# Layer 1 of a four-layer macaron network: gates spread by TensorE row groups, and part of the second mixture's start issued during the attention

## The chip, the cores and the metric

The kernel runs on one core of a Trainium2 chip, in float32. The metric is device time in microseconds (us) of one execution; smaller is better. The engines are TensorE (PE, with its weight loads, PEld), VectorE (DVE), ScalarE (ACT), GpSimd (POOL) and SyncE (SP, which here only issues DMAs). Each has its own instruction queue; they meet at semaphores.

## The reference

The network has four layers. Each is "macaron" shaped: half a feed-forward block, an attention block, half a feed-forward block, all residual, with a layer norm ahead of each. The state x is 4 batches of 512 tokens of 128 values. The feed-forward blocks are mixtures of 8 experts, of four kinds. Only layer 1 is touched by the change. Its mixture is, for normed tokens n:

```
sc   = sigmoid(n @ gate.T)                  # 8 scores per token
m    = the two largest of sc                # top 2
w    = 2.5 * sc[m] / (sum of sc[m] + 1e-20)
y    = sum over the two experts e of w_e * down_e( silu(n @ wg_e.T) * (n @ wu_e.T) )   # inner width 64
y   += the same form with one shared expert of width 128, weight 1
x   += 0.5 * y
```

Its attention is causal, with 16 heads and scores that are the product of two low-rank score matrices (ranks 4 and 8). The same mixture is computed twice, before and after that attention. Layer 2 then follows: a mixture with a linear expert, a gated scan, the mixture again. Layer 3 starts with a mixture that dispatches tokens to experts through DRAM.

## The kernel before

x stays on chip in `xs[b]`, one [128, 4, 128] tile per batch: 128 tokens on the partitions, 4 groups of tokens. Layer 1's mixture computes all 8 experts for all tokens and weighs them by the gates, most of which are zero. Two experts of width 64 fill 128 partitions, so there are `NC` = 4 expert pairs (k = 1 to 4) and the shared expert (k = 0).

`l1_ffn(pool, i, bs)` (L1078) is one mixture for two batches, `bs`; i is 0 for the mixture ahead of the attention and 1 for the one after it. It is a generator: each `yield` is a point at which other work may be put in. Its steps:

- `normed_T` (L1042) norms the batches and turns them with four PE transposes per batch (L187; tile `T_f`), copied to `nT` by ACT (L1049).
- `scored` (L1054, matmul L1058, tile `lg_f`) makes the 8 logits of each token, in groups of 4 small matmuls; ACT makes the sigmoid.
- `up(x, k)` (L1087) makes gate and up projection of one expert pair with two 128x512 matmuls (`gu_f`, L1092 and L1093; each shows as two records), a sigmoid on ACT (L1096) and two products on DVE (L1097, L1098), into a tile `h`.
- `route` and what follows, a chain of small DVE operations, makes `comb`, the weight of each expert for each token (the last step is L1115).
- Tokens must now lie along the free axis, and each expert's weights must be repeated over 64 partitions. `to_rows` (L1067) transposes `comb` to [8, 512] (L1071), copies it out of PSUM with ACT (L1073) and stores it to DRAM (L1075, `rows_f`). Two DMAs per batch (L1124) read it back with a zero step over 64 partitions into `cb` ([128, 4, 512]).
- POOL multiplies each pair's `h` by its slice of `cb` (L1147); `down(k)` (L1132, matmul L1135, tile `o_f`) gathers all five products in PSUM; DVE adds the result to x (L1153).

A mixture takes the batches as two pairs, [0, 1] and [2, 3], whose generators are interleaved by `skewed` with a lag. PE, DVE, ACT and POOL queues are put in order by a scheduler that models the engines, except where the code fixes the order by hand: the attention fixes all four, and the stage after it fixes POOL's. [...]

The first mixture's pair 0 is followed by the begin of the attention for batch 0 (`followed`, L1541): a norm and transposes (`T_a`), matmuls of the low-rank factors (`fac_a`), which go to DRAM and come back rearranged as q and k, and POOL's `k_a` (L1213). The attention (`l1_attn`, L1219) runs 16 units of four heads. When a batch is complete, `ended(b)` adds its projection to x; where a hook `after` is given, its generator for b is then worked off step by step by `go_on`. Before the change layer 1's attention gives no hook.

Behind the attention (`behind`, L1556) each pair runs the second mixture, layer 2's mixture, its scan, its mixture and the start of layer 3's mixture (`f30.tokens`, with indirect DMAs to DRAM on POOL, L408). Layer 2's mixture already spreads its gates with PE: a zeroed tile `l2["gates", …]` is transposed (`gT_f`, L1315), and matmuls of a 0/1 tile with 32 rows (L1346, tile `gate_f`) repeat a row over 128 partitions.

Of the kernel before, what the change touches and what calls it, by code (L numbers as in the profile page):

```python
# [17 lines left out]
P = 128  # L18
# [23 lines left out]
def kernel(ctx: ExitStack, tc: tile.TileContext, a: dict, out: bass.AP):  # L42
# [13 lines left out]
    def bank(name):  # L56
        return psum.tile([P, 512], FP, name=name, tag="bank", bufs=8)
# [954 lines left out]
    def prep_l1():  # L1012
# [26 lines left out]
        l1["wo"] = load_T(a["L1_attn_Wo"], D, D, "wo1T")  # L1039
        l1["bo"] = load_row(a["L1_attn_bo"], "bo1")  # L1040

    def normed_T(pool, bs, tag):  # L1042

        ns = [work.tile([P, NT, D], FP, name=f"n{b}_{tag}", tag="n", bufs=3) for b in bs]
        yield from norms([xs[b] for b in bs], ns, tag, "both")
        nTs = []
        for n, b in zip(ns, bs):
            nT = work.tile([P, S], FP, name=f"nT{b}_{tag}", tag="nT", bufs=4)
            nc.scalar.copy(nT, transposed(n, f"{b}_{tag}"))  # L1049
            nTs.append(nT)  # L1050
        yield
        return nTs

    def scored(nTs, gate, tag):  # L1054

        plg = bank(f"lg_{tag}")
        for t in range(len(nTs) * NT):
            nc.tensor.matmul(  # L1058
                plg[:, t * E : (t + 1) * E],
                nTs[t // NT][:, t % NT * P : (t % NT + 1) * P],  # L1060
                gate,
                start=True,
                stop=True,
            )
        return plg[:, : len(nTs) * NT * E].rearrange("p (g e) -> p g e", e=E)

    def to_rows(pool, gates, i, tag):  # L1067

        pc = bank(f"gT_{tag}")
        for t in range(NT):  # L1070
            nc.tensor.transpose(pc[:E, t * P : (t + 1) * P], gates[:, i * NT + t, :], ident)  # L1071
        gT = pool.tile([E, S], FP, name=f"gT_{tag}", tag="gT")
        nc.scalar.copy(gT, pc[:E, :])  # L1073
        rows = dram.tile([E, S], FP, name=f"rows_{tag}", tag=f"rows_{tag}")
        nc.sync.dma_start(rows, gT)  # L1075
        return rows

    def l1_ffn(pool, i, bs):  # L1078
        tag = f"f1{i}_{bs[0]}"
        G = len(bs) * NT  # L1080
        nTs = yield from normed_T(pool, bs, tag)
        sc = pool.tile([P, G, E], FP, name=f"sc_{tag}", tag="sc1")
        nc.scalar.activation(sc, scored(nTs, l1["gate"], tag), AF.Sigmoid)
        order = [NC] + list(range(NC))
        hs = {}

        def up(x, k):  # L1087
            c = order[k]
            gw = l1["wg"][:, c * P : (c + 1) * P] if c < NC else l1["sg"]
            uw = l1["wu"][:, c * P : (c + 1) * P] if c < NC else l1["su"]  # L1090
            ps = pair(f"gu{c}_{bs[x]}_{tag}")
            nc.tensor.matmul(ps[0], gw, nTs[x], start=True, stop=True)  # L1092
# [5 lines left out]
            nc.vector.tensor_tensor(h, h, ps[1], ALU.mult)  # L1098
# [12 lines left out]

        comb = pool.tile([P, G, E], FP, name=f"comb_{tag}", tag="comb")
        nc.vector.tensor_tensor(comb, m1, m2, ALU.add)
        nc.vector.scalar_tensor_tensor(comb, comb, 2.5, sc, ALU.mult, ALU.mult)
        nc.vector.tensor_tensor(comb, comb, bc(total, [P, G, E]), ALU.mult)  # L1115
        up(0, 1)
        yield
        cbs = []
        for x, b in enumerate(bs):
            rows = to_rows(pool, comb, x, f"{b}_{tag}")  # L1120

            cb = pool.tile([P, NC, S], FP, name=f"cb{b}_{tag}", tag="spread", bufs=4)
            for u in range(2):
                nc.sync.dma_start(  # L1124
                    cb[u * I1 : (u + 1) * I1],
                    bass.AP(tensor=rows.tensor, offset=rows.offset + u * S, ap=[[0, I1], [2 * S, NC], [1, S]]),
                )
            cbs.append(cb)
        for x, b in enumerate(bs):
            po = bank(f"o{b}_{tag}").rearrange("p (t d) -> p t d", d=D)  # L1130

            def down(k):  # L1132

                for t in range(NT):
                    nc.tensor.matmul(  # L1135
                        po[:, t, :],
                        hs[x, k][:, t * P : (t + 1) * P],
                        l1["down"][order[k]],
                        start=(k == 0 and t == 0),
                        stop=(k == NC and t == NT - 1),  # L1140
                    )

            for k, c in enumerate(order):
                if (x, k) not in hs:
                    up(x, k)
                if c < NC:
                    nc.gpsimd.tensor_tensor(hs[x, k], hs[x, k], cbs[x][:, c, :], ALU.mult)  # L1147
                if k > 1:
                    down(k - 2)
                yield  # L1150
            down(NC - 1)
            down(NC)
            nc.vector.scalar_tensor_tensor(xs[b], po, 0.5, xs[b], ALU.mult, ALU.add)  # L1153
            yield
# [61 lines left out]

        return begin, fetch, project, future, {}

    def l1_attn(beside, begun):  # L1219
        begin_, fetch_, project_, future, early = begun  # L1220
        with tc.tile_pool(name="attn1", bufs=2) as pool:
            def begin(b):
                if b == 1:
                    vpads[1] = padded(pool, 1)
                if b > 0:
                    yield from begin_(b)

            def fetch(b, g):
                if (b, g) not in early:
                    fetch_(b, g)  # L1230

            def project(b, g):
                return early[b, g] if (b, g) in early else project_(b, g)

            def residual(b, po):
                nc.vector.tensor_tensor(xs[b], po, xs[b], ALU.add)

            attention(pool, "a1_", begin, project, residual, l1["wo"], lambda h: future, None,
                beside(pool), fetch,
            )  # L1240

# [222 lines left out]
    def whole(parts):  # L1464
        for _ in parts:
            pass
# [57 lines left out]
    with tc.tile_pool(name="weights12", bufs=1) as mid:  # L1524
# [9 lines left out]
        nc.scalar.activation(first, l2["m"][:, 0, 0:1], AF.Sigmoid)  # L1534
        for b in range(NB):
            whole(f01.combine(b))
        with tc.tile_pool(name="ahead1", bufs=2) as ahead:
            vpads[:] = [padded(ahead, 0), None]
            begun = l1_begin(ahead)

            def followed(pool, bs):  # L1541
                yield from l1_ffn(pool, 0, bs)
# [12 lines left out]

        def behind(pool, bs):  # L1556
            yield from l1_ffn(pool, 1, bs)
            yield from l2_ffn(pool, 0, bs)
            yield from l2_attn(pool, bs)
            yield from l2_ffn(pool, 1, bs)  # L1560
            if bs[0] == 0:

                parts = f30.tokens(bs, l3["gate"], "scalar", pool, apart=True)
                while next(parts, "end") != "end" and next(parts, "end") != "end":
                    yield
            else:
                yield from skewed([f30.tokens([b], l3["gate"], "scalar", pool) for b in bs], 3)
# [72 lines left out]
```

## Time and profile before

| What | Value |
|---|---|
| Runs | 1504.74, 1509.73, 1515.06 us; median 1509.73 |
| Profiled execution | 1513.06 us; span 1511.3 us; mean granted PE clock 0.91 |
| PE busy | 1271.2 us (84%) |
| DVE busy | 880.3 us (58%) |
| POOL busy | 694.0 us (46%) |
| ACT busy | 682.8 us (45%) |
| First mixture of layer 1 | about 443 to 513 us of the span |
| Attention of layer 1 | about 515 to 740 us |
| Second mixture of layer 1 | about 740 to 830 us |
| Rest of the stage behind the attention | up to about 1010 us |

The profile is that of one execution. Its page gives the busy time of each engine, groups of instructions (line, engine, operation, tile written and tiles read, how many, busy time, mean of one, and idle time ahead of them with what ended it), and a chain of waits: from the last instruction back to what released it, step by step. "issue" in that chain is time in which an engine waited for nothing that the profile shows. Windows give the busy time of each engine in a stretch, with the clock granted to PE (1.00 is full).

### The profile page before, as it was taken

What the parts mean: (1) busy time and instruction counts of PE and PEld (TensorE: products, weight loads), DVE (VectorE), ACT (ScalarE), POOL (GpSimd) and SP (SyncE); (2) the same over time, 40 slices, a digit from 0 to 9 for tenths busy, and PEclk for the clock granted to TensorE, in tenths of its full rate; (3) what the DMA queues carried; (4) which work ended last, traced back from release to release, by engine and by line L of the source; (5) the groups of instructions that cost most, each with busy time, mean ns of one, the idle gap of its engine ahead of it and who ended that gap; (6) DMA issues with size and microseconds to landing.
All of it is one profiled execution on the core that took longest, in us unless ns stands there. A gap on an engine that the chain in (4) does not pass through costs nothing.

```text
span 1511.3 us, 28774 instructions
## 1 busy us (share of the span) xinstructions
PE 1271.2 (84%) x10645; PEld 816.7 (54%) x10645; DVE 880.3 (58%) x2890; ACT 682.8 (45%) x1431; POOL 694.0 (46%) x808
## 2 busy tenths in 40 slices
PE   4787999995969999999878878729689999998394
PEld 3465666774746666667555656616433333333173
DVE  5236767763355657767456566525367787774343
ACT  1235877871422367767522222103236655564042
POOL 5346767871433678868323111464431223312343
PEclk9897999995999999999999888759879999999597
DMA  9410240002513884231022000023105000000223
GB/s 262 101 53 22 79 170 12 9 7 73 151 37 65 223 258 145 87 121 44 4 64 49 1 1 1 28 71 91 60 15 177 15 7 10 14 3 15 78 78 112
DMA packets 100660, 106.21 MB, mean 70 GB/s; under 512 B 9084, under 2 KB 73832, under 8 KB 100520
## 3 DMA queue, kind: packets, MB, share of 16 engines
q1 hardware_dynamic: 91752, 90.11, 20.7%
q0 software_dynamic: 6656, 13.22, 2.5%
q8 instruction: 84, 1.38, 0.4%
q10 hardware_dynamic: 2112, 1.05, 0.3%
q14 instruction: 56, 0.46, 0.1%
HBM read 62.49 MB, written 41.85 MB: 69 GB/s over the span
## 4 chain that ended last, share of the span: by engine, by line
PE 70%; DVE 9%; POOL 8%; DMA 5%; issue 5%; ACT 3%; SPq 1%; POOLq 0%; ACTq 0%; DVEq 0%
PE s_a L610 13%; PE t_a L655 10%; PE o_f L515 6%; PE h_f L479 6%; PE acc_a L677 5%; PE acc_a L749 5%; PE y_f L1329 3%; PE t_a L610 3%; POOL disp_f L408 2%; PE ot_a L768 2%; PE gu_f L1092 2%; PE lg_f L322 1%; POOL rstd_f L165 1%; DVE low L699 1%; PE gu_f L1093 1%
## 5 line engine op out<-in xcount | busy, mean ns | idle before, releaser
L642 POOL TENSOR_SCALAR sc_a<-sc_a,top_a 128x128 f32<-128x128 f32 (+3 forms) x256 | 274.8, 1089 | 84.7 <-DVE top_a L627 55.8
L610 PE MATMUL s_a<-k_a,q_a 32*128 32x512 f32 (+3 forms) x1536 | 263.4, 544 | 7.0 <-DVE top_a L631 3.7
L719 ACT ACTIVATE w_a<-t_a 128x512 f32<-128x512 f32 x256 | 140.4, 595 | 116.6 <-PE t_a L610 86.9
L699 DVE TENSOR_REDUCE low<-s_a 128x1 f32<-128x512 f32 x256 | 163.4, 684 | 45.4 <-PE t_a L610 32.7
L655 PE MATMUL t_a<-ident,sc_a 128*128 128x128 f32 x1280 | 174.3, 283 | 4.3 <-DVE top_a L631 3.8
L610 PE MATMUL t_a<-ql_a,k_a 32*128 32x512 f32 x512 | 167.2, 644 | 0.3 <-DVE low L699 0.2
L501 POOL DMA_INDIRECT res_f<-y_f,back_f x112 | 109.8, 980 | 124.6 <-ACT y_f L500 90.3
L655 PEld LDWEIGHTS t_a<-ident,sc_a 128*128 128x128 f32 x1280 | 144.6, 144 | 41.0 <-issue 16.5
L644 ACT ACTIVATE sc_a<-sc_a,top_a 128x128 f32<-128x128 f32 (+3 forms) x256 | 135.0, 575 | 12.8 <-DVE top_a L631 12.2
L610 PEld LDWEIGHTS s_a<-k_a,q_a 32*128 32x128 f32 x1536 | 91.5, 187 | 79.1 <-issue 41.9
L664 ACT ACTIVATE w_a<-t_a 128x256 f32<-128x256 f32 (+2 forms) x192 | 94.2, 526 | 71.0 <-PE t_a L655 70.8
L408 POOL DMA_INDIRECT disp_f<-n_f,to_f x96 | 94.8, 988 | 56.2 <-issue 35.8
L515 PE MATMUL o_f<-w_l,h_f 128*128 128x128 f32 (+1 forms) x896 | 109.6, 277 | 0.0
L515 PEld LDWEIGHTS o_f<-w_l,h_f 128*128 128x128 f32 (+1 forms) x896 | 102.1, 184 | 8.0 <-DVE back_f L464 4.4
L479 PE MATMUL h_f<-dT_f,w_l 128*128 128x320 f32 (+1 forms) x256 | 104.1, 544 | 2.8 <-ACT dT_f L457 2.8
L677 PE MATMUL acc_a<-w_a,vpad 128*32 128x128 f32 x2560 | 98.2, 280 | 0.0
L666 ACT COPY w_a<-t_a 128x256 f32<-128x256 f32 (+2 forms) x192 | 93.5, 527 | 5.0 <-PE t_a L655 4.7
L631 DVE CUSTOM_DVE_ANT_0 sc_a<-s_a,future 128x128 f32<-128x128 f32 (+3 forms) x128 | 62.3, 487 | 47.7 <-PE s_a L610 39.0
L1147 POOL TENSOR_TENSOR h_f<-h_f,cb_f 128x512 f32<-128x512 f32 x32 | 40.7, 1286 | 104.4 <-DVE h_f L1098 62.7
L631 DVE CUSTOM_DVE_ANT_0 sc_a<-s_a,table 128x128 f32<-128x128 f32 (+3 forms) x128 | 62.3, 487 | 43.5 <-PE s_a L610 38.3
L500 ACT ACTIVATE y_f<-o_f,d_f 128x128 f32<-128x128 f32 (+1 forms) x112 | 39.0, 394 | 98.0 <-DVE o_f L495 94.1
L749 PE MATMUL acc_a<-w_a,vpad 128*32 128x256 f32 x1024 | 82.1, 391 | 1.0 <-DVE low L699 0.9
(341 smaller groups left out, 2182.8 us busy)
## 6 DMA issues: line engine op xcount, KB each, us to landing
fac_a<-fac_a_sb SPq DMA_DIRECT2D x36, 256.0 KB, 4.9
disp_f<-zeros_f SPq DMA_DIRECT2D x4, 2080.0 KB, 10.6
d_f<-disp_f SPq DMA_DIRECT2D x32, 260.0 KB, 3.0
w_l<-in_L_ffn_w_dram SPq DMA_DIRECT2D x16, 512.0 KB, 7.2
cb_f<-rows_f SPq DMA_DIRECT2D x16, 512.0 KB, 8.4
q_a<-fac_a SPq DMA_DIRECT2D x32, 256.0 KB, 3.5
k_a<-fac_a SPq DMA_DIRECT2D x32, 256.0 KB, 3.8
r_f<-res_f SPq DMA_DIRECT2D x16, 256.0 KB, 2.8
```

The costliest lines, as they stand in the source:

```text
L408: nc.gpsimd.indirect_dma_start(out=self.to[c][i0 + t][:, :], out_offset=bass.IndirectOffsetOnAxis(ap=to[:, c, t : t + 1], axis=0), in_=ns[ ...
L479: nc.tensor.matmul(ps[u][:, :cap], w1[:, e, (c + u) * P : (c + u + 1) * P], dT, start=True, stop=True)
L515: nc.tensor.matmul(po[:m, s, :], h[:, c, s * P : s * P + m], w2[:, e, c, :], start=(c == 0), stop=(c == NC - 1),)
L610: nc.tensor.matmul(ps[:, n0:n1], q[r : r + SLOT, i * P : (i + 1) * P], k[r : r + SLOT, n0:n1], start=True, stop=True)
L631: nc.vector.tensor_tensor_reduce(sc, banks[r][:, :n], more, -1.0, HUGE, ALU.add, ALU.min, top)
L642: nc.gpsimd.tensor_scalar(sc, sc, top, None, ALU.subtract)
L644: nc.scalar.activation(sc, sc, AF.Exp, bias=top, scale=-1.0)
L655: nc.tensor.transpose(ps[:, x * n + j * P : x * n + (j + 1) * P], st["sc", u, i, r0 + x][:, j * P : (j + 1) * P], ident,)
L677: nc.tensor.matmul(st["acc", u][r * SLOT : (r + 1) * SLOT, i * P : (i + 1) * P], vpads[b % 2][:, j, g * 4 + r, :], st["w", u, i, r][:, j * ...
L699: nc.vector.tensor_reduce(st["low", u][:, i, c : c + 1], ps, AX.X, ALU.max, negate=True)
L719: nc.scalar.activation(w, ps, AF.Exp)
L749: nc.tensor.matmul(acc[r * SLOT : (r + 1) * SLOT, n0:n1], vpads[b % 2][:, j, g * 4 + r, :], st["w", u, j, r][:, n0:n1], start=(j == 0 and ...
```

## The change

It has two parts.

The gates of layer 1 are spread by PE instead of a trip through DRAM. The last product of the gate chain is written into a zeroed tile `gates` [128, 8, 128], in which expert e = 2r + u has column 32r + u. `spread(x)` transposes the four [128, 128] blocks of a batch into one bank, ACT copies it to `gT` [128, 512], four matmuls with 32 rows each, one in each of PE's row groups, multiply `halves` (a tile of zeros and ones) by `gT` into four banks, and four ACT copies fill `cb`. It is issued for the pair's first batch ahead of the loop over batches, and for the second at k = 2 of the first batch's loop. The first mixture has a new `gates` tile of its own, zeroed by DVE; the second uses layer 2's. `halves` is built once in a preamble. The stores of rows and the broadcasts go.

The second mixture's pair 0 gets its norms, transposes, `nT` copies and logits in `l1_early`, which runs through the attention's hook for b = 1. Its generator then starts at the sigmoid, with the logits in an SBUF tile that DVE copied from PSUM.

```diff
@@ prep_l1
+        halves = pools["w"].tile([P, P], FP, name="halves", tag="halves")
+        for u in range(2):
+            flag = small.tile([P, 1], FP, name=f"half{u}", tag=f"half{u}", bufs=1)
+            nc.vector.tensor_reduce(flag, ident.rearrange("p (r c) -> p r c", c=SLOT)[:, :, u], AX.X, ALU.add)
+            nc.vector.tensor_copy(halves[:, u * I1 : (u + 1) * I1], flag.to_broadcast([P, I1]))
+        l1["halves"] = halves
...
-    def to_rows(pool, gates, i, tag):
...
+    def l1_early(bs, got):
+        tag = f"f11_{bs[0]}"
+        ns = [work.tile([P, NT, D], FP, name=f"n{b}_{tag}", tag="n", bufs=3) for b in bs]
+        yield from norms([xs[b] for b in bs], ns, tag, "both", True)
+        nTs = []
+        for n, b in zip(ns, bs):
+            yield
+            nT = work.tile([P, S], FP, name=f"nT{b}_{tag}", tag="nT", bufs=4)
+            copy(nT, transposed(n, f"{b}_{tag}"))
+            nTs.append(nT)
+            yield
+        lg = small.tile([P, 2 * NT, E], FP, name=f"lg_{tag}", tag="lg_early", bufs=1)
+        for x in range(len(bs)):
+            yield
+            nc.vector.tensor_copy(lg[:, x * NT : (x + 1) * NT], scored(nTs[x : x + 1], l1["gate"], f"{x}_{tag}"))
+        got[:] = nTs, lg
+
-    def l1_ffn(pool, i, bs):
+    def l1_ffn(pool, i, bs, gates, early=None):
-        nTs = yield from normed_T(pool, bs, tag)
+        if early:
+            nTs, lg = early
+        else:
+            nTs = yield from normed_T(pool, bs, tag)
+            lg = scored(nTs, l1["gate"], tag)
...
-        nc.vector.tensor_tensor(comb, comb, bc(total, [P, G, E]), ALU.mult)
+        parted = gates.rearrange("p g (r c) -> p g r c", c=SLOT)[:, :, :, : E // 4]
+        four = [P, G, 4, E // 4]
+        nc.vector.tensor_tensor(
+            parted, comb.rearrange("p g (r u) -> p g r u", r=4), total.unsqueeze(2).unsqueeze(3).to_broadcast(four), ALU.mult
+        )
...
-            rows = to_rows(pool, comb, x, f"{b}_{tag}")
-            cb = pool.tile([P, NC, S], FP, name=f"cb{b}_{tag}", tag="spread", bufs=4)
-            for u in range(2):
-                nc.sync.dma_start(
...
+        def spread(x):
+            tag_x = f"{bs[x]}_{tag}"
+            pc = bank(f"gT{tag_x}")
+            for t in range(NT):
+                nc.tensor.transpose(pc[:, t * P : (t + 1) * P], gates[:, x * NT + t, :], ident)
+            gT = pool.tile([P, S], FP, name=f"gT{tag_x}", tag="gT2", bufs=2)
+            nc.scalar.copy(gT, pc)
+            cbs[x] = pool.tile([P, NC, S], FP, name=f"cb{tag_x}", tag="spread", bufs=3 + i)
+            banks = [bank(f"cb{r}_{tag_x}") for r in range(NC)]
+            for r in range(NC):
+                rows = slice(r * SLOT, (r + 1) * SLOT)
+                nc.tensor.matmul(banks[r], l1["halves"][rows, :], gT[rows, :], start=True, stop=True)
+            for r in range(NC):
+                nc.scalar.copy(cbs[x][:, r, :], banks[r])
+
+        spread(0)
...
                 if k > 1:
                     down(k - 2)
+                if k == 2 and x + 1 < len(bs):
+                    spread(x + 1)
                 yield
@@ l1_attn
-            attention(pool, "a1_", begin, project, residual, l1["wo"], lambda h: future, None,
+            attention(pool, "a1_", begin, project, residual, l1["wo"], lambda h: future, after,
@@ the stages
+        early = []
...
+                gates = pool.tile([P, 2 * NT, P], FP, name="gates", tag="gates", bufs=1)
+                nc.vector.memset(gates, 0.0)
                 whole(skewed([followed(pool, bs) for bs in pairs], 12))
-            l1_attn(lambda pool: prep_l3_ffn(xs[0]), begun)
+            l1_attn(lambda pool: prep_l3_ffn(xs[0]), begun, lambda b: l1_early(pairs[0], early) if b == 1 else iter(()))
...
-            yield from l1_ffn(pool, 1, bs)
+            yield from l1_ffn(pool, 1, bs, l2["gates", bs[0]], early if bs[0] == 0 else None)
```

More of the change, by code (lines that the diff above doesn't have):

```diff
@@ L1065, in scored @@
         return plg[:, : len(nTs) * NT * E].rearrange("p (g e) -> p g e", e=E)
-    def to_rows(pool, gates, i, tag):
[L1069 to L1076, printed above, removed]
-    def l1_ffn(pool, i, bs):
+    def l1_early(bs, got):
[15 more added lines that the diff above has]
+    def l1_ffn(pool, i, bs, gates, early=None):
         tag = f"f1{i}_{bs[0]}"
         G = len(bs) * NT
-        nTs = yield from normed_T(pool, bs, tag)
+        if early:
[3 more added lines that the diff above has]
+            lg = scored(nTs, l1["gate"], tag)
         sc = pool.tile([P, G, E], FP, name=f"sc_{tag}", tag="sc1")
-        nc.scalar.activation(sc, scored(nTs, l1["gate"], tag), AF.Sigmoid)
+        nc.scalar.activation(sc, lg, AF.Sigmoid)
         order = [NC] + list(range(NC))
@@ L1114, in l1_ffn @@
         nc.vector.scalar_tensor_tensor(comb, comb, 2.5, sc, ALU.mult, ALU.mult)
-        nc.vector.tensor_tensor(comb, comb, bc(total, [P, G, E]), ALU.mult)
+        parted = gates.rearrange("p g (r c) -> p g r c", c=SLOT)[:, :, :, : E // 4]
[3 more added lines that the diff above has]
+        )
         up(0, 1)
         yield
-        cbs = []
-        for x, b in enumerate(bs):
-            rows = to_rows(pool, comb, x, f"{b}_{tag}")
-            cb = pool.tile([P, NC, S], FP, name=f"cb{b}_{tag}", tag="spread", bufs=4)
-            for u in range(2):
-                nc.sync.dma_start(
[L1125 to L1128, printed above, removed]
+        cbs = {}
+        def spread(x):
[13 more added lines that the diff above has]
+        spread(0)
         for x, b in enumerate(bs):
@@ L1217, in l1_begin, with l1_attn @@
         return begin, fetch, project, future, {}
-    def l1_attn(beside, begun):
+    def l1_attn(beside, begun, after):
         begin_, fetch_, project_, future, early = begun
@@ L1541, in followed @@
             def followed(pool, bs):
-                yield from l1_ffn(pool, 0, bs)
+                yield from l1_ffn(pool, 0, bs, gates)
                 if bs[0] == 0:
```

## The prediction

> **What bounds the kernel now.** I read the page first, then the waits of the spread gates, then the chain of waits in the two stretches with layer 1's mixtures, then busy time by stage.
>
> ```profile
> PE 1271.2 (84%) x10645; PEld 816.7 (54%) x10645; DVE 880.3 (58%) x2890; ACT 682.8 (45%) x1431; POOL 694.0 (46%) x808
> ...
> L1147 POOL TENSOR_TENSOR h_f<-h_f,cb_f 128x512 f32<-128x512 f32 x32 | 40.7, 1286 | 104.4 <-DVE h_f L1098 62.7
> ...
> cb_f<-rows_f SPq DMA_DIRECT2D x16, 512.0 KB, 8.4
> ```
>
> ```profile
>   DMA cb_f<-rows_f: 41.6, 3
> ```
>
> TensorE (PE) is the fullest engine, so a gain must remove PE time or PE gaps. POOL's multiply by the spread gates waited for the DMA three times, 41.6 us together; listed singly these were 17.9 us at 464.5 (first mixture), 19.0 at 761.7 and 4.7 at 798.3 (second). POOL has half its time free, so what counts is PE beside these waits.
>
> ```profile
> 450.10 3.83 issue
> 453.93 1.29 PE gT_f L1071 x8
> ...
> 493.45 0.87 PE gu_f L1092 x2
> 496.62 1.15 issue
> 497.77 3.75 POOL h_f L1147 x3
> ...
> 512.91 1.57 POOL h_f L1147
> 514.48 1.23 POOL k_a L1213
> 515.76 1.43 PE s_a L610 x16
> ```
>
> ```profile
> 746.76 4.41 issue
> 752.55 1.46 DMA rows_f<-gT_f
> 754.67 6.85 DMA cb_f<-rows_f
> 761.68 3.71 POOL h_f L1147 x3
> ...
> 791.43 6.77 DMA cb_f<-rows_f
> ...
> 826.96 1.07 PE gate_f L1346 x8
> ```
>
> ```profile
> 454.00:510.00 56.00, 55.57 (x264) 35.49 (x264) 32.25 (x69) 14.83 (x26) 19.98 (x17) 0.97 0.54 138
> ...
> 746.00:752.00 6.00, 1.57 (x8) 0.62 (x7) 4.83 (x21) 0.61 (x2) 0.00 (x0) 0.96 0.00 0
> 752.00:760.00 8.00, 7.93 (x24) 3.78 (x22) 3.01 (x5) 2.85 (x5) 0.00 (x0) 0.82 0.53 135
> 760.00:772.00 12.00, 5.93 (x35) 5.36 (x36) 3.52 (x7) 1.65 (x4) 7.47 (x8) 0.86 0.42 89
> ```
>
> The columns of the last fence are the stretch, its length, busy PE, weight load, DVE, ACT, POOL, then the granted clock. The first mixture (first chain) never shows the DMA: from 454 to 510 PE is busy 55.57 of 56 us, because expert pairs' up-projections were queued ahead of the waiting down-projections. In the second mixture (second chain) the DMA stands on the path twice, 1.46 + 6.85 and 1.43 + 6.77 us, and PE has gaps. Added over 746 to 850, PE is busy 87.5 of 104 us; in the 5-us slices clocks of 0.5 to 0.86 cost about 6 us of the busy time. So some 22 us there are overhead.
>
> **What the Trainium skill says.** "TensorE: Matmul & The Clock Gate", "Measured speedup vs the span model": four row-tiled matmuls (K=32, N=512) are 3.07 times as fast as one by one. The trace agrees: the next layer's gate spread does it, four matmuls (eight records) in 1.07 us in the chain at 826.96, against 3.44 for eight records at the 0.86 per two of L1092. The same page, "What's actually happening": after an idle window of about 3.4 us PE's clock is halved until a busy window has passed. Agrees: after 4.41 us idle a 128x512 matmul took 1.06 us per record against 0.59, and the 5-us slice from 750 had clock 0.66. "TensorEngine Tiling (Array Packing)", "PSUM Bottleneck": after row tiling, the copies out of PSUM may become the bottleneck. Here four ACT copies of 0.6 us follow 1.07 us of matmul; no row of before shows that pressure. "DMA: Bandwidth & Descriptors", "Anatomy of one DMA", puts about 2 us of fixed cost on a DMA, mostly its completion; here 16 KB took 1.46 us and 512 KB 6.85.
>
> **The change, part by part.**
> *Spread by PE.* Removed: 8 stores of rows and 16 broadcasts, 24 issues of SP (0.28 and 0.62 us each; SP is idle enough to count this as zero; the cover is its free queue). Added per batch: the four transposes stay four (0.44 us), but now fill 128 rows; the ACT copy of gT stays 0.57 to 0.60 us; four matmuls 1.07 us; four more ACT copies, 4 x 0.6 = 2.4 us. Over 8 batches PE gets 8.6 us, ACT 19 us. ACT is busy 27 to 33% in the mixtures, so its 19 us is hidden behind PE; without that cover it would be 9.6 per mixture. PE's 4.3 us per mixture lie on the path wherever PE is full. A new wait comes too: PE is served in order, and the four matmuls wait for the gT copy; for each pair's first batch they stand right behind the transposes, with up-projections queued after. That is 0.6 us of copy and two hand-overs, an estimate of 0.8 to 1 us each, twice per mixture; in the second batch a down-projection stands between. The new zeroed gate tile is one DVE memset of 128x1024, at most the 0.92 us POOL takes for the like tile, before the mixture opens. The 0/1 weights are four small DVE instructions (0.25 us) in a preamble: zero, under PE's expert work there.
>
> *First mixture.* No DMA wait is on its path, so nothing is gained by removing it. What ends it is the start of the attention: factor matmuls fac_a (495.0) to DRAM and back to q/k, landed at about 512.8, then k_a on POOL (514.48), first score 515.76. In PE's instruction order before, fac_a stands ahead of the third batch's down-projections; after, these, the spread's matmuls and the fourth batch's come ahead of it. Counting PE's instructions at the durations above, fac_a moves to about 504.5, 9.5 us later. The way from fac_a to q/k, 17.8 us, should lose a little because the 512 KB transfers are gone from it: I take 2. Value +7.5 us; bounds +2.3 (only 4.3 us of PE less 2 us of gap) and +9.
>
> *Moved into the attention.* Norms already ran there. Moved: 8 transposes (0.87), 16 score matmuls (1.70), two nT copies (1.2 of ACT or DVE), two small DVE copies (0.5); no DMA. From 660 to 700 PE is busy 10 of 10, so 2.57 us is on the path if it finds no gap; later in the attention there are small gaps (4.2 of 5 at 700). Bounds 0 and +3; value +1.5.
>
> *Second mixture.* Two accounts. (a) Path: 16.5 us of DMA (sum of the four legs) give way to two times copy 0.6 + matmul 1.07 + copy 0.6 = 4.5, so −12. (b) PE: work of 87.5 us loses the moved 2.6 and gains 4.3, so 89.2; of 22 us overhead about 8 go: the wait of 759.9 to 763 and part of 766 to 772, where batch 0's residual (771.7) moves to about 766, and the half clock after it. What stays: the gate chain on DVE. The sigmoid can start at once, but DVE still has the last residual and the flags of the next layer ahead of it, so the gates are ready only about 1.5 us sooner than 751.07, and PE runs dry at about 743.6 (740.15, the end of the last projection, and four up-projections' 0.86) instead of 746.8, having nothing else. That gives −8 + 1.7 = −6.3. Value −10, nearer the path's because the first multiply comes at about 752 instead of 761.7 and batch 1's at 785 to 790 instead of about 800; bounds −3 and −14.
>
> *After it.* Pair 0 leads, so POOL's queue order changes: pair 0's six dispatch DMAs (L408) for the last layer's mixture (0.99 us each) come ahead of pair 2's norm instead of after. From 850 to 1010 PE is busy 110.8 of 160, so a shift can go either way: 0, bounds −5 and +5.
>
> Sum: 7.5 + 1.5 − 10 + 0 = −1. Against the profiled execution's own 1513.06 us (span 1511.3 and 1.76 around it) that is 1512; this execution lies 3.3 above the median of 1509.73, so I forecast 1509.
>
> **The rivals.**
> *R1: the whole gain arrives.* fac_a's delay is absorbed (POOL waits at 497.77 and 515 to 533 anyway for its own scores) and the second mixture follows its path: 0, +1.5, −14, tail −4: −16.5, 1493. For: 41.6 us of waits vanish and 8.4 MB of traffic. Against: PE's 55.57 of 56 in the first mixture.
> *R2: PE's queue stalls at each spread.* The matmuls wait for the gT copy, which stands on ACT behind sigmoids and earlier spread copies, and everything on PE waits behind them, fac_a among it; POOL then waits, and the next down-projections too. Place: the eight spreads. Price: at 2 us each 16 us, on top of −1 gives +15, 1525; 1% is reached from about 2 us per spread. For: the order puts nothing between transposes and matmuls for each pair's first batch. Against: ACT's low load.
> *R3: the change doesn't do what it says,* the row groups run one after another: 0.86 each, 3.44 per batch instead of 1.07, 8 x 2.4 = 19 us: 1528. Against: the 1.07 us of the same form.
>
> **How the numbers follow.** Forecast (within 1%, which is 15 us, about what a measurement of this kernel tells from no change) 0.62; R1 0.23; R2 0.12; R3 0.03. Adding the ends of the parts gives −20 to +17 around the median, 1490 to 1527; all ends falling together is unlikely, so the range takes R1's and R2's times as its ends: 1493 to 1525. R1 is the faster case, R2 and R3 the slower.
>
> **What would show it.** Right: no wait for a DMA in POOL's multiply; spreads of about 1.07 us; the attention's first score 5 to 9 us later relative to the mixture's start; batch 0 of the second mixture done within 27 us of the last projection instead of 31.5; PE's busy sum up by about 9 us. Wrong: fac_a not later, or the first scores where they were (R1); PE gaps of 2 us ahead of spread matmuls (R2); matmuls at 0.86 apart (R3); or a tail that shifts by over 5 us.

## The result, and the profile after

The changed kernel takes 1520.29 us (median of 13 runs) where the kernel before, on the same chip, takes 1513.35. The ratio is 1.0049, with a 95% interval of 1.0031 to 1.0067: about 7 us slower. The forecast was no change (1509 us). The sign was not forecast, and the parts of the sum were further off than their total.

The profiled execution has a span of 1518.7 us, 7.3 more than before. First, lines of its page: busy time by engine, and the group of POOL's products by the spread gates.

```profile
PE 1282.6 (84%) x10709; PEld 821.8 (54%) x10709; DVE 880.8 (58%) x2898; ACT 700.8 (46%) x1464; POOL 696.0 (46%) x808
...
L1178 POOL TENSOR_TENSOR h_f<-h_f,cb_f 128x512 f32<-128x512 f32 x32 | 40.8, 1275 | 112.4 <-DVE h_f L1116 58.1
```

PE has 11.4 us more to do and ACT 18.0. The second view is that of the spread gates' tile: who works on it, and what POOL waited for.

```profile
L1155 PE MATMUL cb_f<-gT_f,halves x64: 587/692/1218, 457.8 to 805.9; 32*128 32x512 f32 x64
L1157 ACT COPY cb_f<-cb_f x32: 563/592/617, 459.9 to 808.0; 128x512 f32<-128x512 f32 x32
...
  POOL h_f L1178: 31.0, 3
```

POOL's wait for the DMA is gone; in its place stand three waits, 31.0 us together, which ACT's copies end. They are not the price of the copies: of the 31.0 us some 19 had passed before DVE had made the gates, and the rest was transposes, copies and matmuls, each wait ending with the first copy of 0.6 us.

The chain of waits through the first mixture, to set beside the one shown of before:

```profile
452.32 3.74 issue
456.06 1.10 PE gT_f L1148 x4
457.82 2.09 PE cb_f L1155 x8
...
499.64 1.11 PE cb_f L1155 x8
500.75 1.07 ACT cb_f L1157 x3
...
510.55 1.73 PE fac_a L1211 x4
...
522.02 3.67 DMA k_a<-fac_a
526.16 0.88 issue
527.04 1.27 POOL h_f L1178
```

The spread's matmuls are now links of that chain, the attention's factors (`fac_a`) come at 510 instead of 495, and their way through DRAM ends it. The same for the second mixture:

```profile
753.61 4.62 issue
759.65 2.09 PE cb_f L1155 x8
761.74 2.00 PE gu_f L1110 x2
...
768.84 2.03 ACT cb_f L1157 x4
773.03 1.27 POOL h_f L1178
774.42 1.27 POOL h_f L1178
776.11 1.68 POOL rstd_f L165
```

The wait for the gates is still there, 4.62 us where it was 4.41, and no DMA follows. (The view calls it "issue"; DVE finished the gates at 758.1, and PE's transposes of them began at 758.2.) But the chain still passes through POOL.

Four marks divide the two traces: the first score matmul of the first mixture, the attention's first score, its last projection, and the last product of layer 2's two mixtures (`y_f`). In us:

| Stretch | before | after | difference |
|---|---|---|---|
| up to the first mixture | 444.6 | 445.1 | +0.5 |
| first mixture, to the attention's first score | 71.2 | 82.0 | +10.8 |
| attention, to its last projection | 224.4 | 223.0 | −1.4 |
| then to the last `y_f` | 236.5 | 231.4 | −5.2 |
| then to the end | 534.7 | 537.1 | +2.5 |

Each column is one execution. The stretch to the last `y_f` holds the second mixture of layer 1 and layer 2's two; in the last stretch no instruction was changed.

### The profile page after: what moved, and what is told of

Read it like the earlier page. It is cut to its first block, busy times and chain, and to the rows that moved or that the text cites. A ratio compares the mean times of both kernels' runs of the same rounds, so it can differ in the third digit from the quotient of the medians.

```text
span 1518.7 us, 28895 instructions
## 1 busy us (share of the span) xinstructions
PE 1282.6 (84%) x10709; PEld 821.8 (54%) x10709; DVE 880.8 (58%) x2898; ACT 700.8 (46%) x1464; POOL 696.0 (46%) x808
## 3 DMA queue, kind: packets, MB, share of 16 engines
q10 hardware_dynamic: 2112, 1.05, 0.3%
## 4 chain that ended last, share of the span: by engine, by line
PE 69%; DVE 10%; POOL 7%; DMA 5%; issue 5%; ACT 3%; SPq 1%; POOLq 0%; DVEq 0%; ACTq 0%
PE s_a L610 13%; PE t_a L655 9%; PE o_f L515 6%; PE h_f L479 6%; PE acc_a L677 5%; PE acc_a L749 4%; PE t_a L610 3%; PE y_f L1362 2%; POOL disp_f L408 2%; PE ot_a L768 2%; PE lg_f L322 1%; POOL rstd_f L165 1%; PE o_f L1166 1%; PE T_f L187 1%; PE gu_f L1110 1%
## 5 line engine op out<-in xcount | busy, mean ns | idle before, releaser
L610 PEld LDWEIGHTS s_a<-k_a,q_a 32*128 32x128 f32 x1536 | 92.4, 188 | 77.2 <-issue 41.9
L164 POOL TENSOR_SCALAR rs_f<-mv_f 128x4 f32<-128x4 f32 (+1 forms) x23 | 5.5, 239 | 185.1 <-DVE mv_f L161 184.6
```

Source lines behind the costliest of these rows:

```text
L610: nc.tensor.matmul(ps[:, n0:n1], q[r : r + SLOT, i * P : (i + 1) * P], k[r : r + SLOT, n0:n1], start=True, stop=True)
```

## The experiments

Ratios are against the kernel before in runs on the same chip, with 95% intervals; 0.1% is 1.5 us. Two of the four groups of runs (e5 to e8, e13 to e16) fell on two other chips, where the kernel before takes 1535 and 1536 us. The same instructions between the last projection and the last `y_f` took some 12 us longer there (243.5 in e7 against 231.4 in the changed kernel). For the first 219 us of that stretch PE's instructions in these two traces agree within 0.5 us; then comes one stall, which is described at the end. So times inside that stretch are compared over chips only up to the first `y_f`. Ratios differ over chips as well: e8 and e12 are the same kernel and gave 0.9938 and 0.9891. A difference of that size between ratios from different chips is not taken as shown.

### The two parts apart: e1, e2, e3, e5

The theory at this point was the result's own table: the first mixture loses, the second gains, and the early start is small. e1 keeps the spread in the first mixture alone, e2 in the second alone with the early start, e3 has the early start alone, e5 the spread in the second mixture alone. The edit is the same in all, a choice by mixture:

```diff
-        spread(0)
+        if i in SPREAD:                  # (0,), (1,) or ()
+            spread(0)
+        else:
+            for x, b in enumerate(bs):
+                rows = to_rows(pool, comb, x, f"{b}_{tag}")
...
-            l1_attn(lambda pool: prep_l3_ffn(xs[0]), begun, lambda b: l1_early(pairs[0], early) if b == 1 else iter(()))
+            l1_attn(lambda pool: prep_l3_ffn(xs[0]), begun, None)      # e1 and e5
```

> PE spreads the gates in the first mixture only; the second keeps its DMAs, and nothing is moved into the attention. Both theories put the loss into the first mixture, so both expect its first attention score 10 to 12 us later than before (about 526 to 528 of the span instead of 515.8), and the end of the attention about as much later. If the whole of it stays to the end, the kernel is 8 to 12 us slower than before. A rival, that the loss is absorbed by the attention or by the tail, expects less than 4 us.

> PE spreads the gates in the second mixture only, with the early start in the attention; the first mixture is as before. Theory: the first mixture is the loser and the rest a gain. First score at 515 to 517, end of the attention 0 to 2 us earlier than before, the last linear-expert product of layer 2's first stage earlier by about 5 us relative to it, the kernel 4 to 8 us faster than before. Rival: the gain in the second mixture is eaten by the stages after it; then within 2 us of before.

> The early start in the attention alone; both mixtures spread their gates by DMA as before. Expected: the attention's end within 2 us of before (the moved 2.6 us of PE find gaps), the gates of the second mixture's first pair ready about 2 us earlier after the last projection, and the DMA wait after them as long as before, so 1 to 3 us faster. Rival, moved work lies on the attention's full PE: 0 to 2 us slower.

> PE spreads the gates in the second mixture only, and nothing is moved into the attention: the fourth corner of a square whose others are the kernel before, the early start alone and the two together. Theory: the early start and the spread hide the same DMA wait, so alone the spread gains where together it lost 5 us: from the last projection to the last product of layer 2's first stage 229 to 233 us instead of 236.5, the kernel 3 to 7 us faster than before. Rival: the spread costs its PE time whether the wait is exposed or not: 237 to 242 us there, and the kernel 0 to 5 us slower than before.

| Run | first mixture | early start | second mixture | ratio | interval |
|---|---|---|---|---|---|
| e1 | PE | no | DMA | 1.0105 | 1.0076 to 1.0134 |
| e2 | DMA | yes | PE | 0.9974 | 0.9962 to 0.9987 |
| e3 | DMA | yes | DMA | 0.9925 | 0.9901 to 0.9948 |
| e5 | DMA | no | PE | 1.0024 | 1.0006 to 1.0042 |
| changed | PE | yes | PE | 1.0049 | 1.0031 to 1.0067 |

The first mixture was the loser, as expected, and by more: +1.05% alone, 16 us. (Of the 16.0 us between e1's trace and that of before, 9.8 lie in the first mixture and 3.9 behind the last `y_f`, where no instruction differs; why is open.) e2 came out at the lower edge of what was expected. e3 was the miss that turned the study: the part that I had valued at nearly nothing gains 11 us, and e2 against e3, on one chip, says that the PE spread loses 0.49%, 7 us, in the second mixture as well. Their traces agree: from the last projection to the last `y_f` e2 takes 231.2 us, e3 223.7. e5 went to the rival: even where the DMA's wait was exposed, the spread costs 0.24% (3.6 us). From e2 to the changed kernel the first mixture's spread adds 0.75%, where alone it cost 1.05%; what makes that difference is open.

Why nothing came of removing 16.5 us of DMA shows in e5's chain of waits through the second mixture:

```profile
754.58 4.49 issue
...
760.54 2.09 PE cb_f L1171 x8
762.63 2.00 PE gu_f L1123 x2
...
773.86 1.27 POOL h_f L1205
775.55 1.68 POOL rstd_f L165
...
778.34 1.27 POOL h_f L1205
```

After 4.5 us without work PE's clock is low, and the spread takes 2.09 us instead of 1.07 (this is the halving that the Trainium skill describes in "TensorE: Matmul & The Clock Gate", "What's actually happening"). PE then waits 0.68 us for the copy of the transposed gates, and later on POOL's products, between which stands the next pair's norm, as before. In the 100 us after the last projection PE is idle 14.9 us with e5 and 16.7 before; the spread's own 5.2 us more than fill the difference. The first `y_f` comes 92.4 us after the last projection; before it was 90.9.

e11, e3's kernel once more, shows the other side. The first line is POOL's wait for the gates, over both mixtures; then come pieces of the chain of waits through the second:

```profile
  DMA cb_f<-rows_f: 54.4, 4
```

```profile
739.78 4.55 issue
...
746.02 1.46 DMA rows_f<-gT_f
...
748.14 7.16 DMA cb_f<-rows_f
755.46 4.96 POOL h_f L1199 x4
760.85 1.67 POOL rstd_f L165
```

The 54.4 us are not a longer wait than the 41.6 of before: 15.3 of them belong to the first mixture, which is unchanged, and the same wait of before, 15.4 us, is put down to DVE by the view. In the second mixture POOL waits 16.5 and 4.9 us for the DMA, where it waited 19.0 and 4.7. So these waits are nearly all still there, and the kernel is 1% faster. The chain view still lists the DMA, but PE has no gap of 0.1 us from 744.3 to 763.5: while POOL waits, PE makes the second batch's up-projections. Here is PE in the 100 us after the last projection, before and e11 (stretch, length, busy time with records, granted clock, DMA share, GB/s):

```profile
740.15:840.15 100.00, 83.26 (x428) 0.93 0.20 43
```

```profile
736.33:836.33 100.00, 88.36 (x484) 0.95 0.20 44
```

### What sets the first mixture's end: e4, e6, e7, e9

The prediction's theory: the factors fall behind other work in PE's queue, and their way through DRAM sets the first score. The rival: PE's own account (spread matmuls, waits, low clock). e4 and e6 start pair 2 later, which lets the factors pass; e9 begins the attention for batch 0 as soon as that batch leaves the mixture; e7 doubles the spread's matmuls.

```diff
-                whole(skewed([followed(pool, bs) for bs in pairs], 12))
+                whole(skewed([followed(pool, bs) for bs in pairs], 20))      # e4; 16 in e6
```

```diff
+            for _ in range(2 if i == 0 else 1):                              # e7
                 for r in range(NC):
                     nc.tensor.matmul(banks[r], l1["halves"][rows, :], gT[rows, :], start=True, stop=True)
```

```diff
-                yield from l1_ffn(pool, 0, bs, gates)                        # e9
-                if bs[0] == 0:
-                    yield from begun[0](0)
...
+                ffn = l1_ffn(pool, 0, bs, gates)
+                yield from skewed([ffn, attention_begins()], 0) if bs[0] == 0 else ffn
```

> The changed kernel with the second pair of the first mixture started 20 steps behind the first instead of 12, so that PE's queue has the factor matmuls of the attention's first batch ahead of the third batch's down-projections. Theory of the prediction (the late factor chain sets the first score): factor matmuls some 10 us earlier than in the changed kernel, first score at 517 to 519, kernel 8 us faster than the changed one. Rival (PE's own account sets it: spread matmuls, waits behind the gT copy, slow clock): the factors come earlier too, but the first score only by 2 to 3 us, at 523 to 525, and the kernel is 2 to 3 us faster than the changed one.

> The changed kernel with the second pair 16 steps behind, which puts the factor matmuls just after the fourth spread and ahead of the third batch's waiting down-projections. Theory of the prediction (the factor chain sets the first score): first score 8 to 10 us earlier than in the changed kernel, relative to the mixture's first score matmul at 72 to 74 us instead of 82. Rival (PE's own account, with the factor chain worth only the last gap of 2.7 to 3.8 us): 78 to 82 us, and the kernel within 4 us of the changed one.

> The changed kernel with the four spread matmuls of each batch done twice in the first mixture (the second time over the first's result): one cost doubled, 4 times 1.07 us more of PE. If PE's account sets the first mixture's end, the first score comes 4 to 5 us later and the kernel is 4 to 5 us slower than the changed one. If copies on ACT, POOL or the factor chain set it, PE has slack and both move by less than 2 us.

> The changed kernel with the attention's begin for batch 0 started as soon as that batch leaves the first mixture, so that PE's queue has the factor matmuls ahead of the third spread; lag and pairs stay. Theory of the prediction (the factor chain sets the first score): factors at some 45 to 50 us after the mixture's first score matmul instead of 65, first score at 72 to 74 us instead of 82. Rival (PE's own account): factors as early, but the first score at 78 to 80 us, 2 to 4 us better than the changed kernel, since only the last gap of 2.7 us ahead of the first score goes.

From the mixture's first score matmul, in us:

| | factors | attention's first score | ratio to before |
|---|---|---|---|
| before | 50.4 | 71.2 | 1 |
| changed | 65.3 | 82.0 | 1.0049 |
| e4 | 50.9 | 91.2 | 1.0087 |
| e6 | 64.8 | 90.3 | 1.0127 |
| e7 | 71.5 | 88.9 | 1.0088 |
| e9 | 50.2 | 90.3 | 1.0088 |

e4 and e9 have the factors where they were before the change, and the first score is 8 to 9 us later still than in the changed kernel. So early factors are not sufficient, against the prediction's theory, but the rival did not forecast this either. e9's timeline tells why (start, duration, instruction, and in brackets the idle time ahead of it with what ended it). ACT and DVE first, then POOL, then PE:

```profile
511.17 0.65 ACT L1116 ACTIVATE h_f<-gu_f 128x512 f32<-128x512 f32 x1
516.75 0.69 DVE L1249 TENSOR_TENSOR q_a<-q_a,q_a 128x512 f32<-128x512 f32 x1 [3.70 <-DMA q_a<-fac_a]
517.36 0.68 DVE L1117 TENSOR_TENSOR h_f<-h_f,gu_f 128x512 f32<-128x512 f32 x1
...
514.82 1.26 POOL L1249 TENSOR_TENSOR k_a<-k_a,k_a 128x512 f32<-128x512 f32 x1 [6.08 <-DMA k_a<-fac_a]
518.92 1.27 POOL L1249 TENSOR_TENSOR k_a<-k_a,k_a 128x512 f32<-128x512 f32 x1 [2.84 <-DVE h_f L1118]
520.14 2.49 POOL L1180 TENSOR_TENSOR h_f<-h_f,cb_f 128x512 f32<-128x512 f32 x2
...
521.46 2.08 PE L1168 MATMUL o_f<-wd1T,h_f 128*128 128x128 f32 x8 [7.70 <-POOL h_f L1180]
...
538.17 0.48 PE L610 MATMUL s_a<-k_a,q_a 32*128 32x128 f32 x2
```

Once the factors are early, the attention's products come earlier in their engines' queues, too: `q_a` on DVE, `k_a` on POOL. They wait there for their DMAs, and the mixture's products stand behind them. The costly wait was DVE's: a sigmoid that ACT had done at 511.8 got its product on DVE only at 517.4, behind `q_a`; POOL's `k_a` then took 1.3 us more, and PE waited 7.7 us. The factors themselves were no longer the limit: `k_a` was done at 520.2, while PE worked on the mixture without a gap from 521.5 until the first score at 538.2. In e4, too, `k_a` was done at 514.4 and the first score began at 532.8, right behind other work of PE. In e6 the lag delayed the second pair so much that the factors came no sooner; it says nothing on the question.

e7 answers more directly: 4.3 us more of matmuls (at 1.07 us per batch at full clock) move the first score by 6.9 us. Of these, 2.7 had come before the first doubled spread: it began 15.4 us after the mixture's first score matmul instead of 12.7, in an execution whose granted clock up to there was 0.61 instead of 0.75. The other 4.2 are the matmuls' own, so PE has no slack. (The time's 0.39%, 6 us, is taken over two chips.)

The clock is a rival for each difference of a few us here, since each trace is one execution. e3 and e11 are the same kernel, and in both the first mixture is that of before; it took 76.4 and 70.9 us, at a granted clock (the number after the bracket) of 0.89 and 0.98:

```profile
447.50:523.90 76.40, 71.05 (x315) 0.89 0.48 121
```

```profile
443.20:514.10 70.90, 65.28 (x314) 0.98 0.52 130
```

But at 0.98 the first mixture took 71.2 us before and, with the spread, 81.0 in e1, so the spread's loss is not the clock's. The changed kernel's trace shows where it lies. To the end of all its down-projections but the last, PE needs 79.3 us; before, all were done in 71.1. In that, 5.2 us are spread matmuls and 1.4 us two waits behind the copy of the transposed gates; the up-projections took 38.0 us instead of 36.1, and three gaps for POOL's products cost 1.9 where one cost 1.3. In e1 the up-projections took 36.0 us, and the same point came at 77.1. Only then comes a wait for `k_a`, 2.7 us (3.8 in e1), the factors' own share. What stays open is the share of the late factors in a kernel in which DVE's and POOL's order is undisturbed: no run had that.

### Why the early start gains: e10, e13, e14, e15, e16

The early start takes 3 us off the way to the second mixture's gates and 2.6 us of PE off the mixture, yet gains 11 us and more. e10 tested whether the order of up-projections is it, by issuing the second batch's first two ahead of the first batch's downs, in the kernel before:

```diff
+                if i == 1 and x == 0 and k == 0:
+                    for later in range(2, NC + 1):
+                        up(0, later)
+                    up(1, 0)
...
+                if i == 1 and x == 0 and k == 2:
+                    up(1, 1)
```

> The kernel before with one thing added in the second mixture: the second batch's first two up-projections are issued ahead of the first batch's waiting down-projections, as the scheduler came to do by itself with the early start. No work is added or left out. If hiding the DMA under up-projections is most of the early start's gain: from the last projection to layer 2's first product 83 to 87 us instead of 90.9, the kernel 3 to 7 us faster than before. Rival (the gain is the shorter start of the gate chain): within 2 us of before.

It was 1.0058 (1.0043 to 1.0073), slower, and its first `y_f` came at 101.3 us instead of 90.9. The edit reached both pairs, and pair 2's extra up-projections went ahead of pair 0's second batch, which was done at 71.2 us instead of 62.7. That points to the order between pairs. The generator of a pair whose norms were made early has three steps less: two in the norms and one after the transposes. The lag between the pairs stays 8 steps, so pair 0 is three steps further ahead. The next four runs change that lag alone:

```diff
-                whole(skewed([behind(pool, bs) for bs in pairs], 8))
+                whole(skewed([behind(pool, bs) for bs in pairs], 11))        # e13, on the kernel before
```

> The kernel before with one number changed: in the stage behind the attention the second pair starts 11 steps behind the first instead of 8. The early start skips three steps of the first pair (two of the norms, one of the transposes), so it gives the first pair the same lead, and PE's order comes out the same but for the moved instructions. If the lead is most of the early start's gain: from the last projection to layer 2's first product 70 to 74 us instead of 90.9, to its last product 225 to 229 instead of 236.5, the kernel 7 to 12 us faster than before. Rival, the shorter start (3 us) and the moved 2.6 us of PE are the gain: within 3 us of before.

> The early start alone with the lag cut from 8 to 5 steps, so that the pairs stand to each other as before: the moved work without the lead. If the lead is most of the gain: first product at 86 to 89 us, last at 231 to 235, the kernel 1 to 5 us faster than before. Rival: 9 us or more faster, as with the lead.

> The early start alone with 10 steps of lag, a lead larger still. If more lead is better: another 2 to 5 us off, 12 to 18 us faster than before. If the second pair becomes the last: slower than the early start alone at 8.

> The changed kernel with the lag of the stage behind the attention cut to 5 steps: both parts of the change without the lead that comes with them. If the lead is what kept the change near the time of before: 6 to 12 us slower than the changed kernel, 13 to 20 us slower than before. Rival: within 3 us of the changed kernel.

| Kernel | lag | first `y_f` after the last projection, us | ratio | interval |
|---|---|---|---|---|
| before | 8 | 90.9 | 1 | |
| e13: before | 11 | 70.0 | 0.9957 | 0.9943 to 0.9971 |
| e14: early start | 5 | 85.8 | 0.9959 | 0.9947 to 0.9972 |
| e3, e11: early start | 8 | 68.3, 68.4 | 0.9925, 0.9895 | 0.9901 to 0.9948, 0.9863 to 0.9927 |
| e15: early start | 10 | 82.3 | 0.9982 | 0.9966 to 0.9998 |
| changed | 8 | 75.6 | 1.0049 | 1.0031 to 1.0067 |
| e16: changed | 5 | 90.8 | 1.0079 | 1.0057 to 1.0102 |

The lead alone, one number in the kernel before, gains 0.43% (6.6 us by 1536), a little less than expected of it. The moved work without the lead gains 0.41% (6 us), a little more than expected. So neither theory has it all: on one chip each alone is worth some 6 us. That the two add up to the early start's 0.75 to 1.05% is not shown, since the early start at lag 8 was run on other chips only. The first `y_f` says which part brings pair 0 forward: 70.0 us with the lead alone, 85.8 with the moved work alone, 68.3 with both. e16 points the same way, but its 0.30% against the changed kernel, over two chips, is less than e8 and e12 differ by, so the 6 to 12 us expected of it are not shown. More lead isn't better: e15, at 10 steps, is 0.2% slower than e14, at 5, on the same chip, just clear of the noise. It overshoots: pair 2's last batch leaves the mixture 114.7 us after the last projection instead of 89.6 in e3.

### A version that beats both: e8, e11, e12

e8 and e12 are the early start with the gates of pair 0 made in the attention, too (sigmoid as exponential, sum and reciprocal), both mixtures by DMA. e11 and e12 ran on one chip.

```diff
+        nc.scalar.activation(sc, lg, AF.Exp, scale=-1.0)
+        nc.vector.tensor_scalar(sc, sc, 1.0, None, ALU.add)
+        nc.vector.reciprocal(sc, sc)
...
+        nc.vector.tensor_tensor(lg, lg, bc(s1, [P, G, E]), ALU.mult)
```

> The early start alone (gates spread by DMA in both mixtures), carried on: the second mixture's first pair also has its sigmoid (as exponential, sum and reciprocal[...]) and its gates made during the attention. What was left of PE's wait there, 4.6 us ahead of the gates' transposes, goes, and the DMA starts some 8 us earlier. Expected: 3 to 6 us faster than the early start alone, so about 14 to 17 us faster than before. Rival: the added small DVE operations lengthen the attention, or the wait reappears at the first multiply: within 2 us of the early start alone.

> The early start alone once more, beside the version that also makes the gates early, on one chip. Expected again 9 to 13 us faster than before.

> The version with the gates made in the attention too, beside the early start alone on one chip. If its shorter way to layer 2's first product (61.7 us after the last projection against 68.3) reaches the end: 3 to 7 us faster than the early start alone. If the longer attention or the stages after take it back: within 3 us of it.

e8 was 0.9938 (0.9921 to 0.9955), 9.5 us faster than before and not the 14 to 17 expected; e11 was 0.9895, e12 0.9891 (0.9861 to 0.9922). e12's stretch from the last projection to the last `y_f` is 6.6 us shorter than e11's (216.9 against 223.5), but its attention is 2.4 us longer (224.6 against 222.2), and the ratios can't be told apart. The early start alone beats the kernel before by 0.75 to 1.05%, and the changed one by more; what the early gates add is within what these runs tell.

## Why the prediction was wrong

**The step that failed: "Second mixture … Value −10, nearer the path's."** I had two accounts for it, the path's 16.5 us of DMA for 4.5 us of copies and matmuls, and PE's (89.2 us of work instead of 87.5, and some 8 of 22 us overhead gone). The path's account had a sign of its own: batch 0 of the second mixture done within 27 us of the last projection instead of 31.5. Its residual began at 30.4: instead of the DMA, the chain of after leads through the wait for the gates, a spread at half clock and POOL's products. The PE account, −6.3, was close to the −5.2 that the trace shows up to the last `y_f`, and I overruled it. But its closeness is luck: both accounts gave the gain to the wrong part. The spread there costs 3.6 to 7 us (e5; e2 against e3), and the early start makes the gain. The legs of a chain of waits don't add up to what removing them brings: behind the DMA stood POOL's products with the next pair's norm between, and PE's work.

**"Moved into the attention … value +1.5."** The attention was 1.4 us shorter in the changed kernel and 2.1 in e3, which is no more than it varies without the early start (225.4 us in e1, 222.0 in e5): the moved instructions found gaps. All the work that the early start moves is worth −0.41% (e14). I had listed its share, 2.6 us of PE and 1.5 of waiting, but set it within the spread's gain.

**What no step had.** The early start skips three steps of a generator and so shifts the two pairs against each other: worth −0.43% alone (e13). I read the diff's instructions and not the number of its yields. The prediction's last step does say "Pair 0 leads", but only for the order of POOL's queue in the tail, at 0 within −5 and +5.

**"First mixture … Value +7.5; bounds +2.3 … and +9."** The mechanism was half right and the size too small: the first score came 10.8 us later in the mixture, above the bound (9.8 in e1), and e1 makes it 1.05% of the time. The factors were 14.9 us later, not 9.5; their remaining way was 16.7 instead of 20.8 us, so the 2 us taken off for less traffic were 4. The mis-sized term is PE's: I counted 4.3 us of matmuls, and measured 8.2 to the last but one down-projection, 6.0 in e1. The first spread ran at half clock, the waits behind the gates' copy and more gaps for POOL's products came on top, and in the changed kernel's execution the up-projections lost another 1.9 us. `k_a` did come last, but only 2.7 us behind PE's own work. That the factors alone set the first score, as the step says, is not what the runs show.

**Prices.** Four matmuls took 1.06 to 1.14 us at full clock: the 1.07 held, and the row groups did run together, so R3 is out. The spread's wait behind the gates' copy was 0.68 and 0.73 us, close to the 0.8 to 1 estimated; R2's 2 us per spread did not come (one of the eight reached 1.62). The Trainium skill's "TensorEngine Tiling (Array Packing)", "PSUM Bottleneck", says that the copies out of PSUM may become the bottleneck after tiling. They do enter the chain of waits here, with 2.03 us for four (768.84), but they did not become the bottleneck: 5.0 us of PE's waits were for products by these gates (8.6 before).

**R1, the faster case,** had the DMA waits' removal as its reason and falls with it. That 7 us slower lies inside the range from 1493 to 1525 is no merit of the steps: +3.3 of first mixture, −2.9 of attention, +4.8 of second mixture and +2.5 behind it were the errors, by the marks of the table above. The ends of the parts were also added wrongly: as listed they give −16.7 to +14, 1493 to 1524, and not −20 to +17; forecast and range stay as they are.

## What to carry to other kernels

A wait on an engine with time to spare is a price only where the full engine has nothing to do meanwhile; look whether that engine has a gap beside each wait, because here nearly the same DMA waits stood in a kernel that was 1% faster. A wait that the view puts down to one releaser can be put down to another in the next trace, so compare waits one by one and not their totals. Replacing a hidden transfer by work on the fullest engine costs that work, and more where the new work has a hand-over that its queue must wait out. When steps move between interleaved generators, count the yields as well as the instructions: the lead between the two streams is a parameter, and worth a run of its own before a change is judged.

## What the runs showed of the hardware that was not expected

Pulling a product forward made it wait for its DMA in its engine's queue, with work behind it whose inputs were ready: in e9 a DVE product stood 5.5 us behind `q_a`, and PE waited 7.7 us. That is more than the 2.7 us that it was to mend.

The same kernel's first mixture took 76.4 us in one execution and 70.9 in another (e3, e11). In the first, the granted clock was 0.50 for the 9.4 us behind the first score matmul; in the second it was 1.00 there.

The 12 us by which two chips differ up to the last `y_f` are one stall. In e7, from 220.5 us after the last projection on, matmuls of `y_f` come with gaps and a product on DVE stands still, with no releaser that the profile shows; DVE idled 12.67 us. POOL was issuing its 16 indirect DMAs then. In the changed kernel, on the chip of the result, the same instructions run without a gap. What holds them is not shown.
